# Fewer columns picked by VectorE and ScalarE, and fewer rows copied by SyncE, in a graph convolution on one core

## The chip, the core and the metric

The kernel runs on one core of a Trainium2 chip. A core has TensorE (PE, the matrix products), VectorE (DVE), ScalarE (ACT), GpSimd (POOL) and SyncE (SP); each executes its own instructions in order, and they synchronise through semaphores. Transfers run on the core's 16 DMA engines; SyncE, ScalarE and GpSimd issue them. The metric is device microseconds of one execution, less is better. Beside the times there is one profiled execution, with a record of every instruction.

## The reference

There are 12500 nodes with 128 features each and 412500 edges, sorted by their destination node. For every edge the features of the source node are multiplied by weights that a small network makes from eight numbers of the edge, and by four more numbers of the edge; the products are summed by destination.

```
e0 = feat0[edge_src]                      # features of the source node, scalar part
e1 = feat1[edge_src]                      # and vector part
h = gelu(edge_scalar_attr @ W_mlp1 / sqrt(RADIAL))
h = gelu(h @ W_mlp2 / sqrt(HID))
w00, w01, w10, w11 = h @ Wp_00, h @ Wp_01, h @ Wp_10, h @ Wp_11
out0_a = w00 * e0 * ea0
...
n0 = segment_sum(mid0, edge_dst) / sqrt(NUM_NEIGHBORS)
n1 = segment_sum(mid1, edge_dst) / sqrt(NUM_NEIGHBORS)
...
x = layernorm(x + y)
```

What matters here is the first step: for each of the 412500 edges the 128 transformed features of its source node are needed, a row of 512 bytes picked by an index that is only known at run time.

## The kernel before

The edges are cut into runs of 512 (`SB`), 806 runs in all, and a run into four quarters of 128 edges (`Q`). Four runs make a chunk (`CH`). One main loop runs over the step `s`, one run per step; the whole order of work on TensorE, ScalarE, VectorE and SyncE is written out by hand in it, and GpSimd's instructions stand in the order in which the loop creates them.

First the node table is made: `turn` transposes the nodes into `xT` (128 features by 12500 nodes, kept on the chip), `features_of` multiplies them by the weights `wf`, and the result is stored as `table` in the chip's main memory. For the first 18 runs (`RAW`) rows of the input are gathered, and `turn_rows` (line 569 transposes) and `features` transform them in the loop; from run 18 on the rows come from the finished table.

The rows of a run go into a tile `G[s]` of 128 x 4 x 128, of which there are 19 (`LEAD`). At step `s` the loop calls `gather(s + LEAD - 1)`, so rows are fetched up to 18 runs ahead, and a buffer comes free when the products of the run 19 earlier are done. A quarter of a run reaches `G` by one of four ways:

- GpSimd, `gather`, line 220: one indirect DMA takes 128 indices and fetches 128 rows. This is the way of all quarters that no other way takes.
- VectorE, quarter `Q - 2`: `pick_nodes` loads node numbers into registers (line 176), and `pick` copies for each the node's column of `xT` into a tile of 128 columns (line 188, one copy per edge). When 128 columns are there, `picked_rows` multiplies the tile by `wf` on TensorE (line 196), and ScalarE moves the product into `G` (line 197).
- ScalarE, quarter `Q - 3`: the same, with the copies on ScalarE (line 190).
- SyncE, quarter `Q - 1`, in the runs of `aided`: `aid` loads row numbers (line 203) and issues one DMA of 512 bytes per row (line 207), 16 rows (`ROWS`) at a time in eight portions.

`SLOTS` says how many columns an engine picks in each run: VectorE 8, 12 and 12, one group behind each of its three products of the run (`messages(s, part)`: line 602 for part 0, line 606 for parts 1 and 2), so 32 a run and one full tile in four runs; ScalarE 24, 28, 24, 28 and 24 in five runs, so 128, one tile, in five runs. `COL_FROM` gives the run at which picking begins. The table `picked` follows from it: which runs have their quarter filled that way. `AID` is the distance of aided runs, `AID_FROM` the first, `AID_LEAD` by how many steps ahead of it SyncE begins, and `STEPS` over how many steps the eight portions are spread:

```
for t in range(P // ROWS):
    a = s + AID_LEAD - t * STEPS // (P // ROWS)
    if a in aided:
        aid(a, t)
```

In `gather`, a quarter that is picked or aided is left out:

```
if q == Q - 1 and s in aided or any(q == COL_Q[e] and (e, s) in pick_of for e in picked):
    continue
```

Once the rows of run `s` and its weights `WP[s]` (line 560) are there, VectorE multiplies them into `M[s]` in three instructions, and TensorE sums `M` by destination into PSUM (`segments`, lines 631 and 633). Once per chunk VectorE adds the sums to an accumulator (`add`, line 646). When 512 nodes are complete, `moments` makes their output (lines 662 and 665), `statistics` and `normalise` do the layer norm (line 701 is ScalarE's scaling), and SyncE stores the nodes (lines 257 and 259).

Of the kernel before, what the change touches and what calls it, by code (L numbers as in the profile page):

```python
# [15 lines left out]
ACT = mybir.EngineType.Activation  # L16
DVE = mybir.EngineType.DVE
# [25 lines left out]
RAW = 18  # L43
MARGIN = 64
ACC = 768
AID = 14
ROWS = 16
AID_FROM = 36
AID_LEAD = 16
STEPS = 12  # L50
SLOTS = {DVE: [(8, 12, 12)], ACT: [(24,), (28,), (24,), (28,), (24,)]}
COL_Q = {DVE: Q - 2, ACT: Q - 3}
COL_FROM = {DVE: 11, ACT: 16}
LNB = 2


# [1 line left out]
def gnn_kernel(ctx: ExitStack, tc: tile.TileContext, x, src, dst, ea4, ea8, w1_0, w1_1, wm1, wm2,  # L58
# [26 lines left out]
    def sub(ap, offset, dims):  # L85
        return bass.AP(tensor=ap.tensor, offset=ap.offset + offset, ap=dims)
# [24 lines left out]
    G, GT, Y = {}, {}, {}  # L111
    aided = range(AID_FROM, NS - 1, AID)

    slot_at = {}
    for e, cycle in SLOTS.items():
        slot_at[e], n = {}, 0
        for s in range(COL_FROM[e], NS):
            for slot, k in enumerate(cycle[(s - COL_FROM[e]) % len(cycle)]):
                slot_at[e][s, slot] = (n, n + k)
                n += k  # L120

    picked = {}
    for e in SLOTS:
        picked[e] = []
# [6 lines left out]
    pick_of = {(e, s): i for e, g in picked.items() for i, s in enumerate(g)}  # L131
    assert AID_FROM >= raw_runs and AID_LEAD < LEAD and P % ROWS == 0 and STEPS <= AID
    assert all(raw_runs <= g[0] and 0 < len(g) <= 3 * P for g in picked.values())
# [5 lines left out]
    def aid_load():  # L139


        nc.sync.dma_start(aid_at, sub(src, AID_FROM * SB + (Q - 1) * P, [[AID * SB, len(aided)], [1, P]]))
        for e, g in picked.items():
            n = sum(sum(run) for run in SLOTS[e])
            cycle, ahead = n // math.gcd(n, P), P // math.gcd(n, P) * len(SLOTS[e])
            assert all(z - a == ahead for a, z in zip(g, g[cycle:]))
# [697 lines left out]
    with tc.manual_schedule(engines={PE, ACT, DVE, SP}):  # L844
# [49 lines left out]
        for s in range(NCH * CH + CH):  # L894
# [11 lines left out]
# [3 lines that stand above are left out]
# [86 lines left out]
```

## Time and profile before

| what | value |
|---|---|
| median of three runs | 3779.92 us (3772.66 to 3783.14) |
| the profiled execution | 3778.12 us, its span 3776.3 us |
| busy: PE / DVE / POOL / ACT | 3310.0 / 3188.6 / 2678.4 / 2613.7 us |
| mean granted TensorE clock | 0.903 |
| gathers (line 220), table and input | 2742 and 72 |
| copies of columns, VectorE and ScalarE | 25216 and 20096 |
| copies of rows by SyncE | 7040 |

How to read the lines further down. A group's row has line, engine, operation, tiles written and read, shape and count; then busy us and mean ns of one; then the idle time of the engine just before them, with what ended most of it. A row of the waits names who waited for whom, us in total, how often, and the longest. A row in order of time has its start and its length in us; in brackets the idle time before it and what ended that. A row of the windows has the stretch, its length, the busy time with the number of instructions, the granted clock, the share of the DMA engines and GB/s. The chain of work is followed back from the last instruction, at each step to what released it. "issue" means that the engine waited for nothing that the profile shows.

### The profile page before, as it was taken

Reading aid. Unit: us, or ns where it says so; the run is one execution under the profiler, and the core shown is the slowest. Engines: PE = TensorE matmul, PEld = TensorE weight load, DVE = VectorE, ACT = ScalarE, POOL = GpSimd, SP = SyncE. Lnnn points to the kernel's source line nnn. Section 1 sums busy time; section 2 is a strip of 40 time slices with the busy share of each in tenths; the row PEclk is TensorE's granted clock in tenths of the full one; section 3 lists DMA queues with packets and bytes.
Section 4 is the critical chain, followed back from the end, with each engine's and each line's share of the span. In section 5 each row is a group of like instructions: output and inputs, shape, how many; then the busy total and the mean of one; then the engine's idle time right before and its main releaser. Section 6 shows DMA issues by size and latency. Waiting matters only on the chain.

```text
span 3776.3 us, 140497 instructions
## 1 busy us (share of the span) xinstructions
PE 3310.0 (88%) x28568; PEld 2904.3 (77%) x28568; DVE 3188.6 (84%) x28801; ACT 2613.7 (69%) x21733; POOL 2678.4 (71%) x2820
## 2 busy tenths in 40 slices
PE   5888898998898999899898898898898889989888
PEld 4777777777777887787777777777787777878777
DVE  3488898888888899888889888888888888988887
ACT  2377677777676777667767677777777777777775
POOL 7667776777777777677777677677777777767770
PEclk8998898998898899889899899999889889889898
DMA  8223222323222223222233223222322222222220
GB/s 203 48 51 67 60 60 62 63 57 70 61 57 63 63 60 68 61 56 63 61 63 68 58 62 63 58 63 62 68 59 60 60 64 62 61 64 62 58 62 14
DMA packets 579364, 240.07 MB, mean 64 GB/s; under 512 B 483702, under 2 KB 528654, under 8 KB 578510
## 3 DMA queue, kind: packets, MB, share of 16 engines
q0 software_dynamic: 90048, 184.60, 19.1%
q1 hardware_dynamic: 467692, 39.95, 8.7%
q10 hardware_dynamic: 20770, 6.47, 0.7%
q8 instruction: 252, 4.13, 0.4%
q14 instruction: 602, 4.93, 0.4%
HBM read 217.98 MB, written 12.80 MB: 61 GB/s over the span
## 4 chain that ended last, share of the span: by engine, by line
DVE 52%; PE 15%; issue 10%; DVEq 7%; SPq 6%; ACT 5%; DMA 3%; POOL 1%; ACTq 0%; POOLq 0%
DVE gt L188 30%; DVE M L606 14%; DVEq L176 7%; SPq L207 4%; DVE M L602 4%; ACT gt L190 3%; PE sums L631 3%; PE sums L633 3%; PE h L665 2%; PE w L560 2%; PE h L527 2%; DMA G<-table,idx 1%; SPq L203 1%; DVE acc L646 1%; POOL G L220 1%
## 5 line engine op out<-in xcount | busy, mean ns | idle before, releaser
L220 POOL DMA_INDIRECT G<-table,idx x2742 | 2609.0, 952 | 988.0 <-issue 759.6
L190 ACT ACTIVATE gt<-xT 128x1 f32 x20096 | 1970.7, 189 | 318.1 <-issue 316.6
L188 DVE COPY gt<-xT 128x1 f32 x25216 | 1758.2, 144 | 306.8 <-issue 210.3
L633 PE MATMUL sums<-own,M 128*128 128x96 f32 x6446 | 1347.3, 293 | 38.0 <-DVE M L606 37.9
L631 PE MATMUL sums<-own,M 128*128 128x96 f32 x6446 | 1379.6, 298 | 0.0
L631 PEld LDWEIGHTS sums<-own,M 128*128 128x128 f32 x6446 | 1078.5, 207 | 84.4 <-issue 18.7
L633 PEld LDWEIGHTS sums<-own,M 128*128 128x128 f32 x6446 | 1069.5, 208 | 51.6 <-DVE M L606 50.8
L560 PE MATMUL w<-wpb,h 64*128 64x128 f32 x6448 | 722.8, 311 | 269.2 <-DVE M L606 268.2
L560 PEld LDWEIGHTS w<-wpb,h 64*128 64x128 f32 x6448 | 545.6, 201 | 426.9 <-DVE M L606 308.9
L606 DVE TENSOR_TENSOR M<-w,G 128x384 f32<-128x384 f32 x1576 | 861.5, 547 | 0.0
L531 ACT ACTIVATE h<-h 128x512 f32<-128x512 f32 x404 | 216.7, 587 | 226.2 <-PE h L527 215.6
L527 PE MATMUL h<-eT,w1b 64*128 64x128 f32 x3232 | 328.9, 349 | 10.1 <-ACT G L197 7.3
L602 DVE TENSOR_TENSOR M<-w,G 128x256 f32<-128x256 f32 x788 | 321.9, 409 | 10.0 <-ACT G L197 4.0
L527 PEld LDWEIGHTS h<-eT,w1b 64*128 64x128 f32 x3232 | 281.1, 246 | 41.2 <-issue 16.8
L542 PE MATMUL h<-h,w2b 64*64 64x256 f32 x3232 | 248.1, 392 | 3.1 <-ACT h L531 2.6
L197 ACT ACTIVATE G<-h 128x128 f32<-128x128 f32 x354 | 96.2, 272 | 209.0 <-PE h L196 186.8
L547 ACT ACTIVATE h<-h 128x512 f32<-128x512 f32 x404 | 214.4, 580 | 29.5 <-PE h L542 24.3
L196 PE MATMUL h<-wf,gt 128*128 128x128 f32 x708 | 152.0, 298 | 17.1 <-ACT eT L520 14.9
L542 PEld LDWEIGHTS h<-h,w2b 64*64 64x64 f32 x3232 | 117.0, 133 | 62.7 <-ACT G L197 9.9
L595 DVE TENSOR_TENSOR own<-oh,e 128x512 f32<-128x512 f32 x202 | 140.3, 695 | 7.1
L196 PEld LDWEIGHTS h<-wf,gt 128*128 128x128 f32 x708 | 114.0, 203 | 25.2 <-ACT eT L520 23.5
L646 DVE TENSOR_TENSOR acc<-sums,acc 128x384 f32 x202 | 111.1, 550 | 8.5 <-issue 6.2
(112 smaller groups left out, 1232.9 us busy)
## 6 DMA issues: line engine op xcount, KB each, us to landing
G<-table SPq DMA_DIRECT2D x7040, 0.5 KB
G<-table,idx POOLq DMA_INDIRECT x2742
e<-in_edge_attr SPq DMA_DIRECT2D x201, 64.0 KB
xt<-in_x SPq DMA_DIRECT2D x24, 256.0 KB
table<-ft ACTq DMA_DIRECT2D x24, 256.0 KB
xt<-in_edge_attr SPq DMA_DIRECT2D x24, 256.0 KB
out<-y SPq DMA_DIRECT2D x24, 256.0 KB
xt<-in_dst SPq DMA_DIRECT2D x5, 256.0 KB
```

The source lines that it names most:

```text
L176: _, r = nc.values_load_multi_w_load_instructions(pick_rows[e, i][:, r0:r1], engines=[e], min_val=x_at, max_val=x_at + 4 * (N - 1), skip_r ...
L188: nc.vector.tensor_copy(to, col)
L190: nc.scalar.activation(to, col, AF.Copy)
L196: nc.tensor.matmul(pt, GT.pop((e, i)), wf, start=True, stop=True)
L220: nc.gpsimd.indirect_dma_start(out=G[s][:, q, :], out_offset=None, in_=x if s < raw_runs else table, in_offset=bass.IndirectOffsetOnAxis(a ...
L527: nc.tensor.matmul(p1[h][:, j // 2, j % 2, :], w1b[rows, j, :], eT[c][rows, :], start=True, stop=True)
L542: nc.tensor.matmul(p2[r][k * HID:(k + 1) * HID, h * n:(h + 1) * n], w2b[rows, :], H1[c][h][rows, k * n:(k + 1) * n], start=True, stop=True)
L560: nc.tensor.matmul(WP[i][:, q, :], H2[c][q % 2][rows, k, q // 2, :], wpb[rows, :], start=True, stop=True)
L602: nc.vector.tensor_tensor(M[s][:, :, :, :MUL], w[:, :, :2 * MUL].rearrange("p q (a u) -> p q a u", a=2), g[:, :, None, :MUL].to_broadcast( ...
L606: nc.vector.tensor_tensor(M[s][:, :, j, MUL:].rearrange("p q (i u) -> p q i u", i=3), w[:, :, None, (2 + j) * MUL:(3 + j) * MUL].to_broadc ...
L631: nc.tensor.matmul(flat[:, bass.ds(at, 4 * FIRST_HALF)].bitcast(F32), M[s][:, q, 0, :], own[:, 3 * WIDE:], start=False, stop=False)
L633: nc.tensor.matmul(sb[:, 1:, bass.ds(at, 4 * WIDE)].bitcast(F32), M[s][:, q, 1, :], own[:, :3 * WIDE].rearrange("p (a j) -> p a j", a=3), ...
```

## The change

Five constants change. VectorE picks 16 columns a run instead of 32, all behind its last product, from run 7 on instead of 11. ScalarE picks 64 columns in five runs instead of 128. SyncE copies the rows of one run in 28 instead of 14, and its portions are spread over 16 steps instead of 12. The quarters that are no longer picked or aided are gathered by GpSimd through the condition in `gather` above; no other code changes.

```
-AID = 14
+AID = 28
...
-STEPS = 12
-SLOTS = {DVE: [(8, 12, 12)], ACT: [(24,), (28,), (24,), (28,), (24,)]}
+STEPS = 16
+SLOTS = {DVE: [(0, 0, 16)], ACT: [(12,), (12,), (12,), (12,), (16,)]}
...
-COL_FROM = {DVE: 11, ACT: 16}
+COL_FROM = {DVE: 7, ACT: 16}
```

## The prediction

> **What bounds the kernel now.** I read the page's totals, its chain and its groups first.
>
> ```profile
> span 3776.3 us, 140497 instructions
> PE 3310.0 (88%) x28568; PEld 2904.3 (77%) x28568; DVE 3188.6 (84%) x28801; ACT 2613.7 (69%) x21733; POOL 2678.4 (71%) x2820
> DVE 52%; PE 15%; issue 10%; DVEq 7%; SPq 6%; ACT 5%; DMA 3%; POOL 1%; ACTq 0%; POOLq 0%
> L220 POOL DMA_INDIRECT G<-table,idx x2742 | 2609.0, 952 | 988.0 <-issue 759.6
> L190 ACT ACTIVATE gt<-xT 128x1 f32 x20096 | 1970.7, 189 | 318.1 <-issue 316.6
> L188 DVE COPY gt<-xT 128x1 f32 x25216 | 1758.2, 144 | 306.8 <-issue 210.3
> ```
>
> The chain says VectorE: over half of the span is followed back to it, 30% to the column copies of line 188 alone. Whoever stops there expects a large gain from halving them. But line 220, GpSimd's gathers, has 2609 us busy and 760 us idle before it in which nothing that the profile shows was waited for. Whether that is rest or cost, the rows in order of time tell:
>
> ```profile
> 5.00 0.94 POOL L220 DMA_INDIRECT G<-in_x,idx_raw  x1 [0.30 <-issue]
> 6.24 0.94 POOL L220 DMA_INDIRECT G<-in_x,idx_raw  x1 [0.30 <-issue]
> ...
> 200.75 0.94 POOL L220 DMA_INDIRECT G<-table,idx  x1 [0.30 <-issue]
> 209.97 0.94 POOL L220 DMA_INDIRECT G<-table,idx  x1 [8.27 <-ACT h L531]
> ...
> 2001.39 0.94 POOL L220 DMA_INDIRECT G<-table,idx  x1 [0.30 <-issue]
> 2002.64 0.94 POOL L220 DMA_INDIRECT G<-table,idx  x1 [0.30 <-issue]
> ...
> 3688.89 0.94 POOL L220 DMA_INDIRECT G<-table,idx  x1 [0.30 <-issue]
> 3690.14 0.94 POOL L220 DMA_INDIRECT G<-table,idx  x1 [0.30 <-issue]
> ```
>
> Each gather costs 0.94 us and is followed by 0.30 us of nothing, at 5 us, at 2000 us and at 3690 us alike. So the 0.30 belongs to the gather, and GpSimd's price for one is its pitch, 1.25 us, not the 952 ns of the group. The windows, restricted to line 220, give the count (in brackets) beside the length of each stretch:
>
> ```profile
> 0.00:209.90 209.90, 132.93 (x139) 0.92 0.50 116
> 209.90:3691.10 3481.20, 2544.93 (x2675) 0.90 0.29 62
> 1232.00:1520.00 288.00, 218.13 (x230) 0.91 0.29 63
> 2198.00:2428.00 230.00, 174.18 (x184) 0.93 0.28 60
> 3085.00:3306.00 221.00, 167.65 (x176) 0.91 0.29 61
> ```
>
> In the last three stretches, which I chose between GpSimd's waits, the pitch is 288/230 = 1.252, 230/184 = 1.250 and 221/176 = 1.256 us. From 209.9 to 3691.1 us stand 2675 gathers; at 1.255 they need 3357 us of the 3481. GpSimd is therefore 96% taken, and what it really waits for is the other 124 us. The waits name it:
>
> ```profile
> POOL G L220 <- issue: 743.2, 2377, 5.0
> POOL G L220 <- DVE M L606: 111.6, 125, 6.7
> POOL G L220 <- ACT y L701: 16.9, 2, 8.7
> ```
>
> 125 times it waits for a product of line 606, that is for a buffer of G that VectorE has not yet given back. Taking the 0.30 that every gather has out of each, some 74 us are left there and 16 us behind line 701. So VectorE is the bound now, but GpSimd stands only some 190 us behind it: 124 us of waits, and the stretch between its last gather and the end, less what must follow a last gather.
>
> **The change part by part.** Picks and aid take gathers away from GpSimd, one per 128 rows. By the schedule of the changed program VectorE fills 99 such tiles where it filled 25216/128 = 197, ScalarE 78 where it filled 20096/128 = 157, SyncE copies 28 where it copied 55 (the 7040 copies below, divided by 128). That is 205 instead of 409, so the 2742 + 72 = 2814 gathers of now become 2946 + 72 = 3018: 204 more.
>
> ```profile
> G<-table SPq DMA_DIRECT2D x7040, 0.5 KB
> G<-in_x,idx_raw POOLq DMA_INDIRECT x72
> 1999.82 12.37 SPq L207 DMA_DIRECT2D G<-table  x30
> L197 ACT ACTIVATE G<-h 128x128 f32<-128x128 f32 x354 | 96.2, 272 | 209.0 <-PE h L196 186.8
> L196 PE MATMUL h<-wf,gt 128*128 128x128 f32 x708 | 152.0, 298 | 17.1 <-ACT eT L520 14.9
> ```
>
> Taken off VectorE: (197 - 99) x 128 = 12544 copies at (1758.2 + 306.8)/25216 = 0.082 us, 1027 us with the idle time before them. Off ScalarE: 79 x 128 = 10112 at (1970.7 + 318.1)/20096 = 0.114 us, 1152 us, and 177 of the 354 evictions of line 197. TensorE loses half of line 196's 152 us, 76 us. Off SyncE: 27 x 128 = 3456 copies at 12.37/30 = 0.41 us, 1425 us. All of these I cost at nothing. Their cover is GpSimd: VectorE keeps 3188.6 - 12544 x 1758.2/25216 = 2314 busy us, ScalarE 2613.7 - 10112 x 1970.7/20096 - 48 = 1574, and the busiest, TensorE, 3310 - 76 = 3234. None fills the 3018 x 1.255 = 3788 us that GpSimd needs. If TensorE could not keep that pace, the cover would be gone; rival 4 has the price.
>
> Added: 204 gathers x 1.255 = 256 us on GpSimd, which becomes the path. Now the sum. Up to 209.97 us it starts 139 gathers while it waits for the slow first 18 runs, whose rows it gathers raw. VectorE's copies there begin four runs earlier but are half as many a run, and I take that stretch as it is, since the waits in it are for the transposes of raw rows, which stay:
>
> ```profile
> POOL G L220 <- PE h L569: 27.1, 14, 4.7
> ```
>
> As bounds, the 32 us by which it exceeds 3.6 + 139 x 1.255 may all go, or 10 us come. From there 3018 - 139 = 2879 gathers remain, and the last starts 2878 pitches later: 209.97 + 2878 x 1.255 = 3821.9 us. Bounds by the pitch of 1.250 and by that of the whole window, (3481.2 - 120)/2675 = 1.2565: 3807 and 3826 us.
>
> ```profile
> 257.41 2.40 DMA G<-table,idx
> 3668.68 3.56 DMA G<-table,idx
> 3760.33 0.36 DVE L602 TENSOR_TENSOR M<-w,G 128x256 f32<-128x256 f32 x1
> 3770.02 0.47 SPq L259 DMA_DIRECT2D out<-y  x1
> ```
>
> A gather lands 2.4 to 3.6 us after its start; I take 2.9. The last run's products start at 3760.33 now, and the span ends 16.0 us later with sums, normalisation and the store, which must follow in the changed kernel too. TensorE may be a little behind when the last rows come, since the last full group's moments fall there too: 2 us (0 to 4, from none to the length of one run's share of TensorE, 3310/806 = 4.1). Waits of GpSimd that stay:
>
> ```profile
> POOL G L220 <- DVE M L606: 14.3, 22, 4.4
> POOL G L220 <- ACT y L701: 8.2, 1, 8.2
> ```
>
> These are its waits from 209.9 to 800 us. Once it is the slowest, its lead of 18 runs melts and the other engines' bursts no longer stop it; only at the start, with the lead full, can some remain. I take 3 us, with 0 and the 16 us that are left of these rows without their 0.30 each as ends. Sum: 3821.9 + 2.9 + 16.0 + 2 + 3 = 3845.8 us of span. The profiled execution took 3778.12 us for a span of 3776.3, so 1.8 more: 3847.6, call it 3847. It lies 1.8 us below the median of 3779.92, within the spread of the three. Checked the other way: 256 us come, 124 us of waits and 3776.3 - 3690.1 - 18.9 = 67 us at the end take them up, and 65 us are left, 3841.
>
> The new places of the work cost nothing either, with one reserve. VectorE's 16 copies stand in one block behind line 606's second product instead of 8, 12 and 12 between the products: about 1.3 us in a run that GpSimd makes 4.7 us long. With 16 steps instead of 12, SyncE's last 16 rows for an aided run are programmed two runs ahead of it instead of six: 16 x 0.41 = 6.6 us and a landing, against 9.4 us. If a store that waits on SyncE delayed them, a run would stall by a few us, but GpSimd has 18 runs of buffers and would not stop.
>
> **A rule against the trace.** At 5 us, with no column copies running, the pitch is 6.24 - 5.00 = 1.24 us, and amid them at 2001 us it is 2002.64 - 2001.39 = 1.25. So the copies do not slow the gathers visibly. The Trainium skill, SBUF — State Buffer, section "Who interferes with whom", says that a VectorE copy in a two-port mode locks GpSimd out of a port pair that it needs for its descriptors. By that rule half the copies would mean faster gathers; the trace shows at most the 8 ns between the group's mean of 952 and the usual 944, and an estimate by that rule is 2878 x 8 ns = 23 us less, 3824.
>
> **The rivals.**
> 1. Slower, but less: gathers speed up once the copies are fewer. The usual row is 944 ns against the mean of 952, so the whole gain would be 23 us, 3824 us. For it: the slow gathers are strewn over the whole span. Against it: the first of 1.38 us comes at 53.67 us, where no column copy runs yet:
>
> ```profile
> 53.67 1.38 POOL L220 DMA_INDIRECT G<-in_x,idx_raw  x1 [0.30 <-issue]
> ```
>
> Chance 6%; it lies at the range's lower end.
> 2. Faster, the other side: the 0.30 us behind each gather is not the gather's own, but something that lighter traffic of SyncE and VectorE relieves. To end at 3765, the last gather must start by 3741 (3765 less 24), a pitch of (3741 - 210)/2878 = 1.227 instead of 1.255, so the gap would have to shrink from 0.30 to below 0.28 us for every gather. At 0.25 us the span is 210 + 2878 x 1.20 + 24 = 3688. Against it: the gap is 0.30 at 5 us without picks or aid, and at 3690 us after the last aid. Chance 3%.
> 3. No change: the engines that consume stay the bound, and the gathers hide. It would need GpSimd to have 256 us to spare, and it has 124 + 67 = 191. Chance 1%.
> 4. Slower by more: without its lead GpSimd delivers each run just in time, and TensorE, 88% busy, cannot keep 4.7 us a run when landings, aided rows and bursts come on top. Every tenth of a us per run adds 81 us over 806 runs: above 3876, say 3925. For it: a run with all four gathers takes 5.0 us and one with three 3.8, so the supply is uneven. Against it: TensorE's work of 3234 us is 4.0 us a run, and 18 buffers even it out. Chance 6%.
>
> **How the numbers follow.** The forecast has 84%, the rivals 6, 3, 1 and 6%. Forecast: 3847 us. The range must leave out no more than 2 in 10: with rival 1 at its lower end, it reaches from 3826 (pitch 1.250: 3807 + 2.4 + 16 us) to 3876 (pitch 1.2565, 16 us of early waits, 4 us at the end, 3.6 us of landing, and some 10 us of the first stretch); the low end is set to 3822 for rival 1. That holds nearly all of the first two cases. A measurement of this kernel can tell some 0.3%, 11 us, from no change. Faster by more than that: 3%, rival 2. Within: 1%, rival 3. Slower: the rest, 96%.
>
> **What would show it.** Right: 3018 gathers with a pitch of 1.25 to 1.26 us from about 210 us on, hardly a wait behind line 606 after the first hundreds of us, the last gather at about 3822, 70% busy again in a longer span; VectorE near 60% and ScalarE near 41%, idle before line 602 for landings of gathers; the chain through GpSimd with "issue" for its gaps. Wrong: GpSimd's gaps under 0.28 us, or waits behind line 606 that stay at a hundred us, or TensorE as the chain's owner.

## The result and the profile after

The changed kernel takes 3827.57 us (median of four runs, 3822.54 to 3829.49) against 3781.18 us for the kernel before, measured beside it. The ratio is 1.0125, with a 95% interval of 1.0106 to 1.0144. It is 46 us slower; 3847 us had been forecast, with a range of 3822 to 3876.

The page of the changed kernel, totals, chain and the groups that answer to those shown of before:

```profile
span 3824.9 us, 107791 instructions
PE 3318.5 (87%) x28214; PEld 2905.2 (76%) x28214; DVE 2324.0 (61%) x16255; ACT 1659.1 (43%) x11444; POOL 2863.1 (75%) x3024
POOL 39%; issue 26%; PE 16%; DMA 11%; SPq 3%; DVE 3%; ACT 1%; DVEq 1%; ACTq 0%; POOLq 0%
L220 POOL DMA_INDIRECT G<-table,idx x2946 | 2794.4, 949 | 918.0 <-issue 835.8
L602 DVE TENSOR_TENSOR M<-w,G 128x256 f32<-128x256 f32 x788 | 330.4, 419 | 1248.7 <-DMA G<-table,idx 1047.3
L188 DVE COPY gt<-xT 128x1 f32 x12672 | 844.0, 144 | 17.8 <-issue 13.9
```

VectorE has fallen from 52% of the chain to 3%, and GpSimd has risen from 1% to 39%, with another 26% of "issue", most of which lies between two gathers. VectorE now waits 1047 us for gathered rows ahead of a run's first product; in the kernel before it was idle there for 10 us in all. The busy share of GpSimd, 75%, still does not look like a bound. The windows, restricted to line 220, and the waits show that it is one; first the windows of the changed kernel, then those of the kernel before.

```profile
0.00:215.00 215.00, 144.72 (x153) 0.92 0.52 117
215.00:3600.00 3385.00, 2561.69 (x2701) 0.88 0.29 63
```

```profile
0.00:215.00 215.00, 136.75 (x144) 0.92 0.50 114
215.00:3600.00 3385.00, 2476.14 (x2604) 0.90 0.29 62
```

From 215 to 3600 us GpSimd starts 2701 gathers, one per 3385/2701 = 1.253 us, without a break. The waits of GpSimd from 215 us on:

```profile
POOL G L220 <- issue: 811.2, 2661, 0.3
POOL G L220 <- DVE M L606: 17.7, 58, 0.3
```

The longest of each kind is the ordinary gap of 0.3 us. The 111.6 us behind line 606 of the kernel before are gone: GpSimd never waits for a buffer again.

The end, in order of time:

```profile
3802.86 0.94 POOL L220 DMA_INDIRECT G<-table,idx  x1 [0.30 <-issue]
...
3805.35 0.94 POOL L220 DMA_INDIRECT G<-table,idx  x1 [0.30 <-issue]
...
3809.58 0.36 DVE L602 TENSOR_TENSOR M<-w,G 128x256 f32<-128x256 f32 x1
```

The last gather starts at 3805.35 us, the last run's products follow 4.2 us later, and the span ends 15.3 us after that.

### The profile page after: what moved, and what is told of

Same layout as the page of the kernel before. It is cut to its first block, busy times and chain, and to the rows that moved or that the text cites. A ratio compares the mean times of both kernels' runs of the same rounds, so it can differ in the third digit from the quotient of the medians.

```text
span 3824.9 us, 107791 instructions
## 1 busy us (share of the span) xinstructions
PE 3318.5 (87%) x28214; PEld 2905.2 (76%) x28214; DVE 2324.0 (61%) x16255; ACT 1659.1 (43%) x11444; POOL 2863.1 (75%) x3024
## 4 chain that ended last, share of the span: by engine, by line
POOL 39%; issue 26%; PE 16%; DMA 11%; SPq 3%; DVE 3%; ACT 1%; DVEq 1%; ACTq 0%; POOLq 0%
POOL G L220 39%; DMA G<-table,idx 9%; PE sums L631 4%; PE sums L633 4%; PE w L560 3%; SPq L207 2%; PE h L527 2%; DMA xt<-in_x 1%; PE h L542 1%; PE h L665 1%; DVEq L176 1%; DVE M L606 1%; DVE M L602 1%; SPq L203 1%; PE h L577 1%
## 5 line engine op out<-in xcount | busy, mean ns | idle before, releaser
L220 POOL DMA_INDIRECT G<-table,idx x2946 | 2794.4, 949 | 918.0 <-issue 835.8
L631 PE MATMUL sums<-own,M 128*128 128x96 f32 x6446 | 1419.0, 305 | 44.2 <-DVE M L606 43.4
L633 PE MATMUL sums<-own,M 128*128 128x96 f32 x6446 | 1378.1, 299 | 0.2
L631 PEld LDWEIGHTS sums<-own,M 128*128 128x128 f32 x6446 | 1103.3, 212 | 147.9 <-DVE M L606 63.7
L633 PEld LDWEIGHTS sums<-own,M 128*128 128x128 f32 x6446 | 1100.8, 214 | 14.0 <-DVE M L606 13.7
L602 DVE TENSOR_TENSOR M<-w,G 128x256 f32<-128x256 f32 x788 | 330.4, 419 | 1248.7 <-DMA G<-table,idx 1047.3
L190 ACT ACTIVATE gt<-xT 128x1 f32 x9984 | 1016.2, 190 | 45.9 <-issue 34.1
L188 DVE COPY gt<-xT 128x1 f32 x12672 | 844.0, 144 | 17.8 <-issue 13.9
L606 DVE TENSOR_TENSOR M<-w,G 128x384 f32<-128x384 f32 x1576 | 797.0, 547 | 0.0
L520 ACT ACTIVATE eT<-h 128x128 f32<-128x128 f32 x202 | 56.1, 278 | 353.7 <-PE h L518 339.8
L197 ACT ACTIVATE G<-h 128x128 f32<-128x128 f32 x177 | 49.1, 277 | 168.2 <-PE h L196 106.4
L665 PE MATMUL h<-wpost,acc 128*128 128x128 f32 (+1 forms) x784 | 104.1, 276 | 0.0
```

Of the source, the lines that this page charges most:

```text
L188: nc.vector.tensor_copy(to, col)
L190: nc.scalar.activation(to, col, AF.Copy)
L220: nc.gpsimd.indirect_dma_start(out=G[s][:, q, :], out_offset=None, in_=x if s < raw_runs else table, in_offset=bass.IndirectOffsetOnAxis(a ...
L602: nc.vector.tensor_tensor(M[s][:, :, :, :MUL], w[:, :, :2 * MUL].rearrange("p q (a u) -> p q a u", a=2), g[:, :, None, :MUL].to_broadcast( ...
L606: nc.vector.tensor_tensor(M[s][:, :, j, MUL:].rearrange("p q (i u) -> p q i u", i=3), w[:, :, None, (2 + j) * MUL:(3 + j) * MUL].to_broadc ...
L631: nc.tensor.matmul(flat[:, bass.ds(at, 4 * FIRST_HALF)].bitcast(F32), M[s][:, q, 0, :], own[:, 3 * WIDE:], start=False, stop=False)
```

## The experiments

The change sets four constants, `AID`, `STEPS`, `SLOTS` and `COL_FROM`, in three parts: VectorE's, ScalarE's and SyncE's. All times below are medians of several runs; the kernel before, measured on the same chip as each, stands beside them. "Gathers" counts GpSimd's gathers of the whole program.

### VectorE's part undone

```
-SLOTS = {DVE: [(0, 0, 16)], ACT: [(12,), (12,), (12,), (12,), (16,)]}
+SLOTS = {DVE: [(8, 12, 12)], ACT: [(12,), (12,), (12,), (12,), (16,)]}
-COL_FROM = {DVE: 7, ACT: 16}
+COL_FROM = {DVE: 11, ACT: 16}
```

> VectorE picks 32 columns a run again, from run 11 (8, 12, 12), ScalarE and SyncE stay as in the changed kernel: 2920 gathers instead of 3018. Theory (GpSimd's pitch of 1.2534 us is the only bound of the changed kernel): 3827.6 - 98 x 1.2534 = 3705 us if GpSimd stays the bound. Theory's second half (VectorE with 32 copies a run was the bound of the kernel before, whatever the others do): VectorE has the program of before, so about 3770 us, GpSimd waiting some 65 us behind line 606. Rival (the kernel before was bound by ScalarE's or SyncE's share as much): 3705 us.

Measured: 3721.65 us (before 3775.88, ratio 0.9856, 0.9838 to 0.9874). Neither 3705 nor 3770. The second half of the theory falls: VectorE with its old program does not need 3770 us. The chain of this run, its window, and the waits of GpSimd behind line 606 from 215 us on:

```profile
DVE 52%; issue 13%; PE 11%; POOL 10%; DVEq 7%; DMA 5%; ACT 2%; SPq 1%; ACTq 0%; POOLq 0%
215.00:3600.00 3385.00, 2564.80 (x2691) 0.90 0.29 63
POOL G L220 <- DVE M L606: 23.5, 77, 0.3
```

Three waits of VectorE in it:

```profile
DVE rs L688 <- ACT rs L687: 31.0, 13, 3.2
DVE bst L678 <- ACT y L670: 21.2, 11, 3.4
...
DVE M L602 <- DMA G<-table,idx: 12.8, 7, 3.5
```

GpSimd is not held up after 215 us, so its count sets the time: the pitch is 3385/2691 = 1.258 us instead of 1.253, which over some 2770 gathers is 12 us, and the first stretch has 150 gathers instead of 153, 4 us more. That is 16 of the 17 us above 3705. But VectorE waits only 12.8 us for gathered rows, so it is nearly as slow, and the chain, which follows the last releaser at each step, still gives it 52%. In the kernel before, two of these waits, those for ScalarE's results at the end of a group of nodes, are longer:

```profile
DVE bst L678 <- ACT y L670: 59.4, 20, 5.7
DVE rs L688 <- ACT rs L687: 45.8, 13, 4.6
```

That is 53 us more, of the 54 us between the two kernels. So it seems that VectorE together with its waits for a ScalarE that was busy picking held the kernel before at 3776 us. This is read from the waits and not shown: no run removed them alone, and SyncE's part differs between the two kernels too. The wait of line 688 is 43 to 46 us in all four kernels with all of ScalarE's picks whose waits were read (the kernel before, VectorE's part alone, 24 columns, and 28 in one block) and 31 us in the two with half of them, but the one of line 678 does not follow ScalarE's picks so plainly: it is 43.4 us in the changed kernel, with half of them, and 38.6 us in the run with 28 columns in one block further down, with all of them.

### VectorE's part alone

```
-SLOTS = {DVE: [(8, 12, 12)], ACT: [(24,), (28,), (24,), (28,), (24,)]}
+SLOTS = {DVE: [(0, 0, 16)], ACT: [(24,), (28,), (24,), (28,), (24,)]}
-COL_FROM = {DVE: 11, ACT: 16}
+COL_FROM = {DVE: 7, ACT: 16}
```

> Only VectorE's share is halved, from run 7, ScalarE and SyncE as before: 2912 gathers. Theory: GpSimd is the bound with 2912 x 1.2534, so 3827.6 - 106 x 1.2534 = 3695 us, faster than both kernels, with hardly a wait of GpSimd behind line 606. Rival (without VectorE's copies another consumer, TensorE or ScalarE, is at 3770 us too): no faster than 3760 us, GpSimd waiting 70 us.

Measured: 3703.56 us (ratio 0.9811, 0.9795 to 0.9827), 2912 gathers. The theory holds within 9 us, and the pitch, 3385/2700 = 1.254 us, is within a nanosecond that of the changed kernel:

```profile
215.00:3600.00 3385.00, 2561.90 (x2700) 0.90 0.29 64
```

One of the three parts of the change makes the kernel faster by 72 us; ScalarE's and SyncE's parts on top, 106 gathers more, make it slower by 124 us, where 106 x 1.2534 = 133 had to be expected.

### 24 columns a run

```
-SLOTS = {DVE: [(8, 12, 12)], ACT: [(24,), (28,), (24,), (28,), (24,)]}
+SLOTS = {DVE: [(8, 8, 8)], ACT: [(24,), (28,), (24,), (28,), (24,)]}
```

> VectorE picks 24 columns a run (8, 8, 8) from run 11, ScalarE and SyncE as before: 2863 gathers. Theory: GpSimd's sum is 3827.6 - 155 x 1.2534 = 3633 us; VectorE loses 49 x 128 copies at 0.082 us, 514 us of the 3776, so it is no bound; 3633 to 3660 us with some waits left. Rival (TensorE, 3310 us busy, has a floor of its own): 3690 to 3720 us, with GpSimd waiting 60 to 90 us.

Measured: 3658.71 us (ratio 0.9688, 0.9672 to 0.9704), 2863 gathers, at the upper end of the theory's range. There is no floor of TensorE at 3690 us. The sum was 26 us short, and the window accounts for it:

```profile
215.00:3600.00 3385.00, 2566.16 (x2685) 0.92 0.29 64
```

The pitch is 3385/2685 = 1.261 us, 7.5 ns above that of the changed kernel, though GpSimd waits no more here. On 2718 gathers that is 20 us; and up to 215 us it starts 145 gathers instead of 153, another 10 us, together a little more than is missing. So a gather's price is not quite constant, which the next two runs take up.

### Copies without fewer gathers

The changed kernel, with every one of VectorE's column copies made twice into the same column:

```
 nc.vector.tensor_copy(to, col)
+nc.vector.tensor_copy(to, col)
```

> The changed kernel, each of VectorE's column copies made twice into the same place: 25344 copies again, but still 3018 gathers. Theory (copies do not touch the gathers, and VectorE in the shadow costs nothing): 3827 us within 0.3%, pitch 1.253 us. Rival (copies slow the gathers: 1.2566 us a gather amid the copies of before against 1.2534 in the changed kernel): pitch back at 1.2566 us, 2868 x 3.2 ns = 9 us more, 3837 us. Rival (VectorE near its limit stalls the chain): 3850 us and more.

Measured: 4853.63 us (ratio 1.2852, 1.283 to 1.2873). This tested something else than it was meant to. VectorE's rows in order of time:

```profile
2001.46 0.15 DVE L188 COPY gt<-xT 128x1 f32 x1
2001.65 0.15 DVE L189 COPY gt<-xT 128x1 f32 x1
2001.72 0.14 DVE L188 COPY gt<-xT 128x1 f32 x1
2001.89 0.15 DVE L189 COPY gt<-xT 128x1 f32 x1
```

A copy into the column that the copy before it wrote starts 0.17 to 0.19 us later, the next one to another column 0.07 us after that. A pair takes 0.25 us, where two independent copies of the changed kernel take 2 x 844.0/12672 = 0.13. Sixteen pairs are 4.0 us of a run, and VectorE becomes the bound. So the copies went into a tile of their own that nothing reads:

```
 nc.vector.tensor_copy(to, col)
+nc.vector.tensor_copy(spare_cols[:, spare_n[0] % P:spare_n[0] % P + 1], col)
+spare_n[0] += 1
```

> The changed kernel with each of VectorE's copies followed by one of the same column into a spare tile that nothing reads: 25344 independent copies as in the kernel before, 3018 gathers. Theory (VectorE lies in GpSimd's shadow, and each independent copy costs it some 0.07 us): VectorE near 3170 us busy, time 3827 us within 0.3%. Rival (copies slow the gathers): the slow gathers come back to the 20 to 33 us over 0.944 us each that the kernels with many copies show, 14 us in the changed kernel, so 3834 to 3846 us. Rival (it is the length of VectorE's block behind the products that stalls the chain, as in the run with copies into the same place): above 3850 us.

Measured: 3843.5 us (before 3771.26, ratio 1.0187, 1.016 to 1.0214), and 3842.2 us of span where the changed kernel had 3824.9, on a chip on which the kernel before is 10 us faster than beside the changed kernel. VectorE's 12672 extra copies cost 17 us or somewhat more, not the 844 us of their own time: VectorE does lie in GpSimd's shadow. But they are not free. The window of this run, and the group of its gathers:

```profile
215.00:3600.00 3385.00, 2565.69 (x2687) 0.89 0.28 62
```

```profile
L223 POOL DMA_INDIRECT G<-table,idx x2946 | 2811.8, 954 | 917.6 <-issue 819.6 <-DMA G<-table,idx 38.1 <-PE h L572 19.0
```

The pitch is 3385/2687 = 1.260 us instead of 1.253; 2865 gathers x 6.5 ns = 19 us. The rival holds, with one reserve: copies slow the gathers, by half a percent, but the changed kernel was not run on this chip. Three runs that share a chip point the same way: the pitch is 1.254 us with 16 of VectorE's copies a run (VectorE's part alone), 1.261 with 24 and 1.258 with 32 (VectorE's part undone). The first two of them differ in nothing but VectorE's picks. It is not the number of copies alone, since 24 lengthen the pitch more than 32. The run with copies into the same place made as many as this one, and its gathers took 946 ns in the mean, but there GpSimd also stood idle behind VectorE's copies for 930 us:

```profile
L221 POOL DMA_INDIRECT G<-table,idx x2946 | 2788.3, 946 | 1862.2 <-DVE gt L188 929.5
```

### The copies' place

```
-SLOTS = {DVE: [(0, 0, 16)], ACT: [(12,), (12,), (12,), (12,), (16,)]}
+SLOTS = {DVE: [(4, 6, 6)], ACT: [(12,), (12,), (12,), (12,), (16,)]}
```

> The changed kernel with VectorE's 16 copies split 4, 6 and 6 behind the three products of a run instead of all behind the last; the same 3018 gathers. Theory (the place of the copies is free): 3827 us within 0.3%. Rival (copies between the products bring the slow gathers, 20 to 33 us over 0.944 us in the three kernels that split them, 14 us in the two that do not): 3834 to 3846 us.

Measured: 3836.19 us (ratio 1.0169, 1.0143 to 1.0195). That is within 0.3% of the changed kernel and also within the rival's 3834 to 3846, so the time alone does not decide. Measured by the kernel before beside each, the two are 1.0169 and 1.0125, 0.4% apart, and their intervals just touch. The count speaks for the rival: 2693 gathers in the window of 3385 us, a pitch of 1.257.

```profile
215.00:3600.00 3385.00, 2563.73 (x2693) 0.88 0.29 62
```

### 28 columns a run

The kernel before with 28 columns, in three groups and in one:

```
-SLOTS = {DVE: [(8, 12, 12)], ACT: [(24,), (28,), (24,), (28,), (24,)]}
+SLOTS = {DVE: [(8, 10, 10)], ACT: [(24,), (28,), (24,), (28,), (24,)]}
```

> VectorE 28 columns a run (8, 10, 10) from run 11, ScalarE and SyncE as in the kernel before: 2839 gathers, 24 fewer than with 24 columns. Theory (GpSimd still the bound): 3658.7 - 24 x 1.2609 = 3628 us, the fastest of all. Rival (VectorE and its waits for ScalarE already bind): above 3665 us.

Measured: 4898.86 us (ratio 1.2988, 1.2963 to 1.3014), where 3628 had been expected and the rival said 3665 or more. The miss has a place. Line 176 loads the node numbers of a group into VectorE's registers. Three loads of one run, and one of 12 numbers in the kernel before (the three numbers are the least, the median and the longest in ns):

```profile
L176 DVEq TENSOR_LOAD <-pick x1: 600/600/600, 2008.0 to 2008.0; - x1
L176 DVEq TENSOR_LOAD <-pick x1: 1068/1068/1068, 2009.0 to 2009.0; - x1
L176 DVEq TENSOR_LOAD <-pick x1: 2293/2293/2293, 2010.5 to 2010.5; - x1
```

```profile
L176 DVEq TENSOR_LOAD <-pick x1: 849/849/849, 2009.5 to 2009.5; - x1
```

Eight numbers take 0.60 us and twelve 0.85, but ten take 1.07 us in one place and 2.29 in the other. A run's loads are 3.96 us together, and VectorE, which cannot copy what is not loaded, is held to 6 us a run: 4891/806 = 6.07. Its wait for that stands in its group:

```profile
L188 DVE COPY gt<-xT 128x1 f32 x22016 | 1565.1, 145 | 1688.1 <-issue 1670.6
```

Why ten numbers load so slowly was not tried. The traces give a hint: the three loads start 0, 8 and 18 numbers into the run's 28. In the run with 4, 6 and 6 columns they start at 0, 4 and 10 and take 0.35, 0.83 and 1.45 us. In both, the slowest is the one whose start is no multiple of four, with 2.29/10 = 0.23 and 1.45/6 = 0.24 us a number, where eight numbers in 0.60 us are 0.075 each. No run moved the start alone. With one group of 28:

```
-SLOTS = {DVE: [(8, 12, 12)], ACT: [(24,), (28,), (24,), (28,), (24,)]}
+SLOTS = {DVE: [(0, 0, 28)], ACT: [(24,), (28,), (24,), (28,), (24,)]}
```

> As the run with 28 columns in (8, 10, 10), but all 28 behind the last product: 2839 gathers. Theory (place free): the same time as that run within 0.3%. Rival (copies in one block spare the gathers): pitch 1.254 instead of 1.261 us, 20 us faster than with (8, 10, 10), 3608 us. Rival (28 copies ahead of the next run's first product hold it up by 2 us): slower than with (8, 10, 10).

Measured: 3626.51 us (before 3771.26, ratio 0.9615, 0.9593 to 0.9636): 3628 had been worked out for GpSimd as the bound. It is the fastest version, 4% ahead of the kernel before and 5% ahead of the changed one, and GpSimd is still never held up after 215 us:

```profile
POOL G L220 <- issue: 715.4, 2344, 0.3
POOL G L220 <- DVE M L606: 32.3, 106, 0.3
```

The comparison of one block with three groups is lost to the loads.

### Four runs that tell nothing of the change

The last four ran together on a chip on which the kernel before took 5569.25 us.

```
-SLOTS = {DVE: [(8, 12, 12)], ACT: [(24,), (28,), (24,), (28,), (24,)]}
+SLOTS = {DVE: [(0, 0, 32)], ACT: [(24,), (28,), (24,), (28,), (24,)]}
```

> The kernel before with VectorE's 32 copies all behind the last product instead of 8, 12 and 12; 2814 gathers as before. Theory (VectorE with 32 copies a run and its waits is the bound of the kernel before, wherever the copies stand): 3771 us within 0.5%. Rival (it was the place of the copies, and GpSimd binds again): 25 gathers fewer than with 28 in a block, 3626.5 - 25 x 1.258 = 3595 us.

```
-STEPS = 16
+STEPS = 12
```

> The changed kernel with SyncE's portions spread over 12 steps again instead of 16; 3018 gathers. Theory (SyncE's spread is hidden by the buffers): 3827.6 us within 0.3%. Rival (the last portion comes late in the changed kernel): faster by some us for each of 28 aided runs, 3800 us or less.

```
-AID = 28
+AID = 14
-STEPS = 16
+STEPS = 12
```

> The changed kernel with SyncE's part undone, one run in 14 and 12 steps: 2991 gathers. Theory: 3827.6 - 27 x 1.2534 = 3794 us. Rival (SyncE's rows contend with the gathers): less of a gain, above 3805 us.

> The run with 12672 spare copies once more, beside the changed kernel with 12 steps on one chip. If copies slow the gathers, 16 us above that kernel again; if the 16 us were the difference of two chips, within 0.3% of it.

Measured, in this order: 5575.54, 5759.78, 5887.02 and 5623.53 us, that is 1.0016 (0.9991 to 1.0041), 1.034 (1.0299 to 1.0381), 1.0566 (1.0526 to 1.0607) and 1.0103 (1.0059 to 1.0147) of the kernel before there. The bound was another one on that chip. The waits of the run with 12 steps, which is the changed kernel but for SyncE's spread:

```profile
POOL G L220 <- DVE M L606: 1330.4, 298, 16.8
...
PEld sums L631 <- issue: 346.5, 581, 2.6
PE sums L631 <- issue: 223.4, 258, 2.5
```

GpSimd waits 1330 us for buffers, and TensorE's weight loads of line 631 stall for 346.5 us with no cause that the profile shows, where the changed kernel has 24.5. The granted clock was 0.719, in the changed kernel 0.883. None of these runs can test a theory on GpSimd's pace, and no verdict is drawn. So it stays open what 32 copies in one block do, what SyncE's spread alone is worth, and whether SyncE's part alone follows the sum. That the run with spare copies, with 16 steps, is faster there than the one without them, with 12, is unexplained.

## Why the prediction was right

**The bound.** That VectorE was the bound of the kernel before, with GpSimd close behind, was right and is shown: with GpSimd given 98 gathers more and VectorE relieved, the kernel gains 72 us; with 204 more it loses 46. That VectorE's copies alone were the bound was too simple: the first experiment gives VectorE its old work and is still 54 us faster, with shorter waits for ScalarE.

**The count and the price.** The 3018 gathers came exactly. The price of 1.255 us, gap included, measured 1.253; the mean of 952 ns on the page would have given the change some 60 us less. GpSimd's 75% busy is the share that this price implies, 949/1253 = 0.76; the 70% that the prediction named as a sign was not worked out from it. That the 0.30 us gap belongs to the gather stands: it is 0.30 us at 3803 us too, with VectorE at 61% and SyncE done. Rival 2, the only faster one, falls with that.

**The cover.** VectorE has 2324 us busy (2314 worked out), ScalarE 1659 (1574), TensorE 3318 (3234; the granted clock was 0.883 instead of 0.903). The last two lost about 85 us less than worked out. None became a bound, so the edits costed at nothing cost nothing that the profile shows; rival 4 and rival 3 fall. SyncE's spread was not tested by itself.

**The terms that were mis-sized.** The span came out at 3824.9 instead of 3845.8 us, and the terms account for it:
- "I take that stretch as it is": the first 215 us. There GpSimd started 153 gathers instead of 144; once its early waits are over, it is 12 us ahead of the sum. The bound of this term allowed it, the value did not, and its reason fails: the waits behind line 569 did not stay, they fell from 27.1 to 21.2 us, and the 8.27 us ahead of the gather at 209.97 us, which are put down to line 531, became 3.29 us ahead of one at 203.11 us. Those two are 11 us. It may be that ScalarE's picks stood ahead of the raw runs' evictions and halved; in ScalarE's rows of the kernel before, line 571 comes behind a block of copies:

```profile
197.86 0.74 ACT L190 ACTIVATE gt<-xT 128x1 f32 x7
199.40 0.60 ACT L571 ACTIVATE xt<-h 128x512 f32<-128x512 f32 x1 [0.79 <-ACT gt L190]
```

  But the run with only VectorE's part undone starts 150 gathers in this stretch and the one with VectorE's part alone 151, so either side by itself brings most of the nine, and which copies were in the way is not shown.
- The pitch: 1.2534 instead of 1.255 over some 2865 gathers, 5 us less.
- The waits that were to stay: none instead of 3 us.
- Landing and end: 4.2 + 15.3 us instead of 2.9 + 16.0 + 2, 1.4 us less.

**The rule and the trace.** The sentence that the copies "do not slow the gathers visibly" was too strong. The Trainium skill, SBUF — State Buffer, section "Who interferes with whom", says that VectorE's copies in a two-port mode can hold GpSimd up, and the run with spare copies agrees in direction: 6.5 ns a gather, 19 us, within the 23 us that the prediction gave as the most. It does not agree as a lock would have it for each copy, since 12672 copies of 144 ns cost GpSimd 19 us in all; whether copies of one column run in that mode no run shows. Rival 1, gathers that speed up with fewer copies, was thus the case in part: the mean gather fell from 952 to 949 ns, 3 of its 8 ns or some 9 of its 23 us, and the pitch that fell short of the forecast is 5 us.

## What to carry to other kernels

When work moves from the engine that the chain names to another, count the instructions that the other one gets and price them by the distance from start to start, not by the busy time of one; then compare with what that engine has to spare, its waits plus its lead at the end. Here it could spare some 190 us, and 256 came. When the two bounds cross, a better point can lie between; the best of the versions tried has an eighth of VectorE's copies given up, the rest in one block, and ScalarE's and SyncE's left alone. It took 3627 us, while the whole change gave 3828.

## What the runs showed of the hardware

Two VectorE copies of 128 x 1 in a row to different columns follow each other in about 0.07 us; a copy into the place just written waits until 0.17 to 0.19 us after the first one's start. A load of eight numbers into VectorE's registers took 0.60 us and one of twelve 0.85, but loads of ten took 1.07 or 2.29 us; how numbers are grouped for loading can cost more than what is done with them. And dense copies on VectorE go with a longer pitch of GpSimd, 1.258 to 1.261 us instead of 1.253; how, these runs do not show.
